# A ConvNeXt block and two Mamba layers on one core: a smaller first convolution group, ordered ahead of the weight preparation, and half of the first MLP moved into the stages

## The chip, the cores and the metric

The kernel runs on one core of one Trainium2 chip. A core has a matrix engine (TensorE, PE in the profile, with its weight loads as PEld), a vector engine (VectorE, DVE), a scalar engine (ScalarE, ACT) that evaluates functions such as exp or GELU from tables, a general engine (GpSimd, POOL) and a queue engine (SyncE, SP) that only issues DMA transfers. ACT and POOL can issue transfers too. Every engine takes its instructions in order and waits for the others through semaphores. The metric is the device time of one execution in microseconds; lower is better.

## What is computed

The input is `x` of 32 batches, 96 channels, 56 by 56 pixels, in fp32. Two layers follow each other.

```python
# layer 0, per batch
h = depthwise_conv7x7(x) + conv_b            # each channel with its own 7 x 7 filter
h = layernorm over the 96 channels
h = gelu(h @ w1 + b1) @ w2 + b2              # 96 -> 384 -> 96
x = x + layer_scale * h
# layer 1: two Mamba blocks over the 3136 pixels of a batch as a sequence
for i in range(2):
    xs, z = split(layernorm(seq) @ in_w[i])                  # 96 -> 2 x 192
    xc = silu(causal_conv4(xs))
    dt, Bm, Cm = split(xc @ xproj_w[i])                      # 6, 16, 16
    delta = softplus(dt @ dt_w[i] + dt_b[i])
    state = exp(delta * A) * state + delta * Bm * xc         # along the sequence, 192 x 16 states
    seq = seq + ((sum(state * Cm) + Dp * xc) * silu(z)) @ out_w[i]
# global branch, fusion, batch norm over all batches, and the residual
gp = relu(mean(x) @ gp_w.T + gp_b)
out = batchnorm(fus_w @ concat(seq, gp) + fus_b) + x
```

## The kernel before

**Front.** The depthwise convolution is done on PE. For a pair of channels, a banded matrix made of the filter (tile `band`, 112 rows by 7 times 128 columns) is multiplied with the padded image rows of the pair (`xpad`, 112 rows by batches by 62), in 7 matmuls, one per column shift, that add up in one PSUM bank. The bands are made by one trick: `line` (one row per channel, on DVE) is written 14 times over to `band_d` in DRAM (L137), and `load_band` (L154) reads it back with a row pitch one shorter than it was written. `conv_pair` issues the loads of `xpad` (L171) and `band`, the matmuls (L178), the evacuation to `ct` on ACT with the bias `cb` (L183) and the store to `conv_d` (L184). All these transfers are issued by SP. Three `band` and three `xpad` tiles rotate. The first group has 8 batches, so a matmul has 448 columns; its 48 pairs run in the front.

Between pair 2 and pair 3 stands, in the source, the preparation of the weights: small loads issued by POOL, products on DVE, three matmuls at L270 (`norm_weights`) and nine at L299 and L306, and two exponentials on ACT (`ar`, L327). The framework's scheduler orders the front itself, by its own estimates, so the order on an engine is not that of the source: on PE, L270, L299 and L306 stand ahead of the first conv pair. A transfer uses one of eight semaphores in turn (separately for POOL's and for those of SP and ACT), and waits until the transfer that had that semaphore before has landed.

Behind the conv comes the first MLP, for batch 0 alone: `block0(b, c, s)` is one half (392 pixels) of one chunk (784 pixels) of a batch, 8 halves a batch. In a half, the conv result `cv` is loaded (L417) and normalised (`center`, `square`, `mean`, `root`, `norm`: L379, L384, L389, L395/L396, L446), goes through both matrices with GELU between them (L451, L459, L467/L471), and the residual (L477) is stored to `x1_d` (L481). All eight halves of batch 0 run in the front from two pools of their own (`p0`, `pp0`), two halves at a time.

**Stages.** The rest is 256 stages, one for each layer, batch and chunk, in an order written out by hand (`manual_schedule`): layer 0 of a chunk, layer 0 of the next, layer 1 of the first, and so on. A stage has 24 steps; each step is an exponential on ACT (L918), a product with B (L900, DVE), a scan on DVE (L975), a product with C on POOL (L980), and matmuls that spread the input over the states (L947) and add the states up (L1021). Around the steps, pieces of other work are put by slot numbers, 24 slots a stage: `prep` of the next stage, `post` of the one before, one `block0` half of a later batch and one `conv` pair of a later group.

```python
        for m, S in enumerate(stages):
            ...
            if 2 <= m < len(halfs) + 2:
                put(m, block0(*halfs[m - 2]))
            if 2 <= m < len(convs) + 2:
                put(m, conv(*convs[m - 2]))
            if m + 1 < len(stages):
                put(m, prep(stages[m + 1]))
```

So conv pairs of the four later groups (6 batches each, 192 pairs) are in stages 2 to 193, and halves of batches 1 to 31 in stages 2 to 249. In a `conv` pair of a stage, loads are at slot -0.5, the taps (L565) at 5.4 to 10.2, the store at 11.8. A half loads `cv` at slot -6 and has its residual at 18.8. The matmuls of the first `prep` run ahead of the first step, and the first spread waits for the projection of the second stage's `prep` (L635), which stands in front of it on PE.

At the very end, statistics over all batches are reduced and the output is made from `o_d` and `x1_d` (the `fin` loop).

Of the kernel before, what the change touches and what calls it, by code (L numbers as in the profile page):

```python
# [34 lines left out]
F32 = mybir.dt.float32  # L35
# [7 lines left out]
H = W = 56  # L43
L = H * W
C = 96
# [6 lines left out]
NCH = 4  # L52
# [6 lines left out]
HP = 64  # L59
REP, PER = 14, 1024  # L60
# [3 lines left out]
def convnext_mamba_kernel(  # L64
# [31 lines left out]
    nc = tc.nc  # L96
    B = x.shape[0]

    dram = ctx.enter_context(tc.tile_pool(name="dram", bufs=1, space=DRAM))
    const = ctx.enter_context(tc.tile_pool(name="const", bufs=1))  # L100


    NB = 6
    b0 = B - 4 * NB if B > 4 * NB else B
    groups = [(0, b0)] + [(b, min(b + NB, B)) for b in range(b0, B, NB)]
    conv_d = [
        dram.tile([C * HP, (hi - lo) * W], F32, name=f"conv_d{lo}", tag=f"conv_d{lo}")
        for lo, hi in groups
    ]
    band_d = dram.tile([C, REP * PER], F32, name="band_d")  # L110
    stats_d = dram.tile([C, B * NCH, 4], F32, name="stats_d")
    x1_d = [dram.tile([C, L], F32, name=f"x1_d{b}", tag=f"x1_d{b}") for b in range(B)]
    o_d = [dram.tile([C, L], F32, name=f"o_d{b}", tag=f"o_d{b}") for b in range(B)]
# [3 lines left out]
    P2 = 2 * HP  # L117
    M2 = HP + H
    cb = const.tile([P2, C // 2], F32, name="cb")
    first_conv = ExitStack()  # L120
    cc = first_conv.enter_context(tc.tile_pool(name="cc", bufs=1))
    cx = first_conv.enter_context(tc.tile_pool(name="cx", bufs=3))
    cps = first_conv.enter_context(tc.tile_pool(name="cp", bufs=6, space=PSUM))
    cw = cc.tile([C, 49], F32, name="cw")
    nc.sync.dma_start(cw, conv_w)
    line = cc.tile([C, PER], F32, name="line")
    nc.vector.memset(line, 0.0)
    for dh in range(7):
# [3 lines left out]
            line.rearrange("p (k n) -> p k n", n=P2)[:, 0:7, HP + H + 2 - dh],  # L132
            cw[:, 7 * dh : 7 * dh + 7],
        )
    for lo in range(0, C, 24):
        r = slice(lo, lo + 24)
        nc.sync.dma_start(  # L137
            band_d[r].rearrange("c (r n) -> c r n", n=PER),
            line[r].unsqueeze(1).broadcast_to([24, REP, PER]),
        )  # L140
    nc.vector.memset(cb, 0.0)
    bv = conv_b.rearrange("(p two) k -> two p k", two=2)
    for j in range(2):
        nc.sync.dma_start(
            cb[j * HP : j * HP + H].unsqueeze(2), bv[j].partition_broadcast(H)
        )

    def load_band(T, p):

        for j in range(2):
            w = band_d[2 * p + j]
            nc.sync.dma_start(  # L154
                T[j * H : (j + 1) * H],
                bass.AP(
                    w.tensor, w.offset + HP + H - 1 - HP * j,
                    [[PER - 8, H // 8], [PER - 1, 8], [1, 7 * P2]],
                ),
            )  # L160

    bands, xpads = [], []
    for i in range(3):
        t = cc.tile([R2, 7 * P2], F32, name=f"band{i}", tag=f"band{i}")
        bands.append(t)
        t = cc.tile([R2, b0, W + 6], F32, name=f"xpad{i}", tag=f"xpad{i}")
        nc.gpsimd.memset(t, 0.0)
        xpads.append(t)
    def conv_pair(p):
        xp, T = xpads[p % 3], bands[p % 3]  # L170
        nc.sync.dma_start(  # L171
            xp[:, :, 3 : 3 + W],
            x[0:b0, 2 * p : 2 * p + 2, :].rearrange("b c (h w) -> (c h) b w", w=W),
        )
        load_band(T, p)
        ps = cps.tile([M2, b0 * W], F32, name="ps")
        for dw in range(7):
            nc.tensor.matmul(  # L178
                ps, T[:, dw * P2 : dw * P2 + M2], xp[:, :, dw : dw + W],
                start=(dw == 0), stop=(dw == 6),  # L180
            )
        ct = cx.tile([M2, b0 * W], F32, name="ct")
        nc.scalar.activation(ct, ps, AF.Identity, bias=cb[0:M2, p : p + 1])  # L183
        nc.sync.dma_start(conv_d[0][p * P2 : p * P2 + M2, :], ct)  # L184

    for p in range(3):
        conv_pair(p)


# [15 lines left out]
    for a in range(2):  # L205
        r = slice(64 * a, 64 * a + 64)
# [67 lines left out]
    for i in range(2):  # L274
# [12 lines left out]
        xp = blocks(xproj_w[i], f"xq{i}", su)  # L287
# [58 lines left out]
        nc.vector.memset(t[C : C + 1, :], 1.0)  # L346
        hn0s.append(t)

    for p in range(3, C // 2):
        conv_pair(p)  # L350
    first_conv.close()


    with ExitStack() as main:
        pre = []
# [49 lines left out]
        batch_sums = {}  # L405

        def block0(b, c, s):
            k = c * 2 + s
            v = {}

            def load():
                if k == 0:
                    batch_sums[b] = work([C, NCH * 2], "sums", 2)
                v["cv"] = work([C, ROWS, W], "cv", 1)
                g = 0 if b < b0 else 1 + (b - b0) // NB
# [97 lines left out]
        with tc.tile_pool(name="p0", bufs=1) as p0, tc.tile_pool(  # L513
            name="pp0", bufs=1, space=PSUM
        ) as pp0:
            pre += [p0, pp0]
            pieces = [
                (slot + 4 * c, piece)
                for c in range(NCH)
                for s in range(2)  # L520
                for slot, *_, piece in block0(0, c, s)
            ]
            for _, piece in sorted(pieces, key=lambda p: p[0]):
                piece()
            exp_ln_tables()
            pre.clear()
# [341 lines left out]
        stages = []  # L868
        for i, b, c in order:
            S = Stage()  # L870
            S.i, S.b, S.c, S.d, S.da, S.e, S.h, S.u4, S.pb = i, b, c, lay[i], {}, {}, {}, {}, {}
            stages.append(S)
        convs = [(g, p) for g in range(1, len(groups)) for p in range(C // 2)]
        halfs = [(b, c, s) for b in range(1, B) for c in range(NCH) for s in range(2)]

        def wide(k):

# [152 lines left out]
        def put(m, pieces):  # L1030
            for slot, *piece in pieces:
                where = slots if len(piece) == 1 else within
                where.setdefault(m * NSTEP + math.floor(slot), []).append((slot % 1, piece[-1]))
# [61 lines left out]
    with tc.tile_pool(name="sp", bufs=1) as sp:  # L1095
        n = B * NCH
# [21 lines left out]
    with tc.tile_pool(name="fin", bufs=4) as fin:  # L1118
        for b in range(B):
            for a in range(2):  # L1120
# [3 lines left out]
                r = fin.tile([C, 2 * CH], F32, name="fr")  # L1124
# [63 lines left out]
```

## Time and profile before

| | us |
|---|---|
| median of 3 executions | 15764.34 |
| lowest and highest | 15749.59, 15781.1 |
| the profiled execution | 15761.56 |
| its span in the profile | 15759.8 |

| engine | busy us | share |
|---|---|---|
| PE | 13461.7 | 85% |
| PEld | 5646.6 | 36% |
| DVE | 14771.9 | 94% |
| ACT | 11966.7 | 76% |
| POOL | 14367.3 | 91% |

The profile's page gives the busy time of each engine over the span, and rows of 40 equal slices (394 us each) in which a digit is the busy share in tenths. The timeline has one row per group of instructions: start in us, duration in us, engine, source line, operation, written tile, read tiles, shapes, count, and in brackets the idle time before it with what ended it. A row marked SPq is a transfer that SP's queue issued, and its duration is the time to issue it, with the time that the queue stood on it. A row of stretches gives the busy time of PE, PEld, DVE, ACT and POOL with the number of instructions, the granted TensorE clock (1.00 is full speed), the share of the 16 DMA engines' time, and GB/s.

### The profile page before, as it was taken

The numbers are of one execution on the slowest core, as the hardware profiler recorded it, in microseconds if no ns is written. First come the engines' busy times: TensorE is split into PE (matmuls) and PEld (weight loads), VectorE is DVE, ScalarE is ACT, GpSimd is POOL, SyncE is SP. The second block draws the span as 40 slices with busy tenths as digits, with TensorE's granted clock in tenths as the row PEclk, the third lists the DMA queues.
The fourth block names the chain that finished last, engine by engine and source line by source line (L and its number), as shares of the span: only waits on it lengthen the run. The fifth ranks groups of instructions, "written<-read, shape, count | busy, mean of one in ns | idle before, by whom it ended". The sixth has DMA issues, their size and how long they took to land. (4 is left out here: it accounts for less than half of the span.)

```text
span 15759.8 us, 207713 instructions
## 1 busy us (share of the span) xinstructions
PE 13461.7 (85%) x72120; PEld 5646.6 (36%) x72120; DVE 14771.9 (94%) x11457; ACT 11966.7 (76%) x23091; POOL 14367.3 (91%) x4746
## 2 busy tenths in 40 slices
PE   7798888888898898888898888998888888888870
PEld 3333333333333333333333333333333333333320
DVE  0799999999999999999999999999999999999993
ACT  1677778777878777787777787787777777777763
POOL 0799999999999999999999999999999999999990
PEclk9899999999999999999999999999999999999985
DMA  4454555555555545455554545545444444444438
GB/s 126 126 155 150 154 150 153 155 150 152 152 155 153 150 147 157 150 154 150 152 156 149 154 150 154 155 150 153 150 150 140 139 136 143 137 140 137 142 121 295
DMA packets 1304619, 2381.45 MB, mean 151 GB/s; under 512 B 490094, under 2 KB 699374, under 8 KB 1303564
## 3 DMA queue, kind: packets, MB, share of 16 engines
q1 hardware_dynamic: 1294108, 2327.73, 48.5%
q10 hardware_dynamic: 7168, 38.54, 0.6%
q8 instruction: 568, 9.31, 0.2%
q14 instruction: 487, 3.99, 0.1%
q0 software_dynamic: 2288, 1.88, 0.1%
HBM read 1973.83 MB, written 393.81 MB: 150 GB/s over the span
## 5 line engine op out<-in xcount | busy, mean ns | idle before, releaser
L980 POOL TENSOR_TENSOR h<-h,cp 128x1568 f32<-128x1568 f32 x3072 | 9939.7, 3251 | 547.1 <-DVE h L975 484.4
L975 DVE TENSOR_TENSOR_SCAN h<-da,w 128x785 f32<-128x785 f32 (+1 forms) x3072 | 5390.1, 1776 | 2.0 <-ACT da L918 2.0
L975 DVE TENSOR_TENSOR_SCAN h<-w,h 128x785 f32<-128x785 f32 (+1 forms) x3072 | 5287.1, 1769 | 73.0 <-ACT w L918 63.9
L957 POOL TENSOR_TENSOR h<-us,bp 128x1570 f32<-128x1570 f32 x1024 | 3323.7, 3246 | 73.3 <-PE y L1021 26.4
L918 ACT ACTIVATE w<-d,A 128x784 f32<-128x784 f32 x3072 | 2819.3, 918 | 576.9 <-DVE h L975 492.9
L900 DVE TENSOR_TENSOR w<-w,bp 128x786 f32<-128x786 f32 x3072 | 2916.4, 980 | 212.6 <-PE w L947 93.8
L918 ACT ACTIVATE da<-d,A 128x784 f32<-128x784 f32 x3072 | 2890.3, 947 | 12.4 <-DMA d<-dd 11.6
L1021 PE MATMUL y<-h,ssum 128*32 128x392 f32 x24576 | 2611.8, 516 | 39.7 <-POOL h L980 38.2
L635 PE MATMUL ps<-hn,wx 97*64 97x392 f32 x12288 | 2206.7, 501 | 22.0 <-POOL hn L626 22.0
L947 PE MATMUL w<-u,sel 64*128 64x393 f32 x4096 | 1002.0, 565 | 1173.9 <-DVE h L975 1160.1
L917 ACT COPY w<-st 128x1 f32<-128x1 f32 x2304 | 372.4, 162 | 1281.7 <-DVE h L975 1248.5
L565 PE MATMUL ps<-xpad,band 112*120 112x336 f32 x2688 | 1060.1, 512 | 331.4 <-ACT dl L708 331.4
L1021 PEld LDWEIGHTS y<-h,ssum 128*32 128x32 f32 x24576 | 698.6, 111 | 1724.1 <-issue 1488.3
L635 PEld LDWEIGHTS ps<-hn,wx 97*64 97x64 f32 x12288 | 813.8, 136 | 1348.5 <-issue 1291.5
L900 DVE TENSOR_TENSOR h<-w,bp 128x786 f32<-128x786 f32 x1024 | 990.5, 967 | 0.0
L375 ACT ACT_TABLE_LOAD x759 | 973.8, 1283 | 14.2 <-PEq L1175 0.7
L947 PEld LDWEIGHTS w<-u,sel 64*128 64x128 f32 x4096 | 327.2, 191 | 1565.8 <-DVE h L975 1140.8
L930 PEld LDWEIGHTS y<-sel 128*128 128x128 f32 x6144 | 747.1, 192 | 259.0 <-issue 97.0
L930 PE MATMUL y<-sel 128*128 128x120 f32 x6144 | 794.6, 279 | 21.1 <-DVE z L996 21.1
L384 ACT ACTIVATE sq<-ps 96x392 f32<-96x392 f32 x768 | 378.7, 493 | 557.6 <-PE ps L379 392.7
L565 PEld LDWEIGHTS ps<-xpad,band 112*120 112x120 f32 x2688 | 449.6, 191 | 935.2 <-ACT dl L708 446.5
L626 POOL TENSOR_TENSOR hn<-seq,hn 96x784 f32<-96x784 f32 x256 | 472.5, 1846 | 337.2 <-ACT hn L396 337.2
(158 smaller groups left out, 15975.4 us busy)
## 6 DMA issues: line engine op xcount, KB each, us to landing
d<-dd SPq DMA_DIRECT2D x1536, 392.0 KB
bp<-bd SPq DMA_DIRECT2D x1024, 392.0 KB
cp<-bd SPq DMA_DIRECT2D x1024, 392.0 KB
us<-uu SPq DMA_DIRECT2D x512, 392.0 KB
dd<-dl SPq DMA_DIRECT2D x512, 294.0 KB
band<-band_d SPq DMA_DIRECT2D x480, 196.0 KB
uu<-u SPq DMA_DIRECT2D x1024, 49.0 KB
cv<-conv_d SPq DMA_DIRECT2D x256, 147.0 KB
```

The costliest lines, as they stand in the source:

```text
L375: nc.scalar.preload_act_table_set("natural_log_exp_and_others")
L565: nc.tensor.matmul(v["ps"][0:M2, 0 : nb * W], band[:, dw * P2 : dw * P2 + M2], xpad[:, 0:nb, dw : dw + W], start=(dw == 0), stop=(dw == 6),)
L626: nc.gpsimd.tensor_tensor(hn, S.seq, hn, ALU.mult)
L635: nc.tensor.matmul(v["x", q][rows(a), 0:HC], weights[:, k, 64 * q : 64 * q + 64], v["hn"][:, o : o + HC], start=(k == 0), stop=(k == last),)
L900: nc.vector.tensor_tensor(halves(S.pb[j, g]), halves(S.u4[j])[:, :, 0 : HC + 1], halves(S.bc[0, g // 2][:, g % 2, :]), ALU.mult,)
L918: nc.scalar.activation(e[:, 1 : 1 + CH], S.d4[j], AF.Exp, scale=S.d["A"][:, j, g : g + 1])
L930: nc.tensor.matmul(spare, sel[:, 0, :], sel.rearrange("p a b -> p (a b)")[:, 0 : 512 - HC], start=True, stop=True,)
L947: nc.tensor.matmul(u4[:, 512 * a : 512 * a + HC + 1], sel[rows(a), j % 2, :], S.u[rows(a), j // 2, a : a + HC + 1], start=True, stop=True,)
L957: nc.gpsimd.tensor_tensor(states(S, j, h)[:, :, 0 : 1 + CH], S.us[j].unsqueeze(1).broadcast_to([128, 2, 1 + CH]), S.bc[0, h][:, :, 0 : 1 + ...
L975: nc.vector.tensor_tensor_scan(h[:, g % 2, at], S.e.pop((j, g))[:, at], S.pb.pop((j, g), h[:, g % 2, :])[:, at], 1.0 if c else 0.0, ALU.mu ...
L980: nc.gpsimd.tensor_tensor(h[:, :, 0:CH], h[:, :, 1 : 1 + CH], S.bc[1, g // 2], ALU.mult)
L1021: nc.tensor.matmul(S.y[r0 : r0 + 32, 0:HC], ssum, hs[k][:, g, tok(a)], start=False, stop=(half == 1 and g == 1),)
```

## The change

- The first group has 6 batches instead of 8; the later ones 6, 6, 7 and 7 instead of four of 6. A conv matmul of the front has 336 columns; one of the last two groups has 392.
- In the source, 24 conv pairs instead of 3 stand ahead of the weight preparation. After the other 24, the first five pairs of the second group run in the front too.
- `band` and `xpad` have six tiles each instead of three, `ct` six buffers instead of three.
- The bands are written in three parts: channels 0 to 7, 8 to 31 and 32 to 95, the last two when `conv_pair` comes to pairs 2 and 8.
- The bias `conv_b` is loaded as one row to all partitions (by ACT's queue) and sorted into `cb` by two DVE copies, instead of two loads of single elements by SP.
- The front's stores of `ct` are issued by ACT instead of SP.
- Of batch 0, four halves (chunks 0 and 1) of the MLP run in the front instead of eight. Half (0, 2, 0) is put into the `prep` of the first stage, halves (0, 2, 1) and (0, 3, 0) into stage 0, and (0, 3, 1) into stage 2. Each later half comes one stage later than before.
- The conv pairs of the stages start in stage 0 instead of stage 2: 187 pairs in stages 0 to 186.

```diff
-    NB = 6
-    b0 = B - 4 * NB if B > 4 * NB else B
-    groups = [(0, b0)] + [(b, min(b + NB, B)) for b in range(b0, B, NB)]
+    b0 = NB = min(6, B)
+    EARLY = 5
+    groups = [(0, b0)]
+    while groups[-1][1] < B:
+        lo = groups[-1][1]
+        groups.append((lo, min(lo + NB + (lo >= 3 * b0), B)))
+    NB = max(hi - lo for lo, hi in groups)
...
-    band_d = dram.tile([C, REP * PER], F32, name="band_d")
+    chunks = ((0, 8), (8, 32), (32, C))
+    band_d = [
+        dram.tile([hi - lo, REP * PER], F32, name=f"band_d{lo}", tag=f"band_d{lo}")
+        for lo, hi in chunks
+    ]
...
-    cx = first_conv.enter_context(tc.tile_pool(name="cx", bufs=3))
+    cx = first_conv.enter_context(tc.tile_pool(name="cx", bufs=6))
...
-    for lo in range(0, C, 24):
-        r = slice(lo, lo + 24)
+
+    def write_bands(k):
+        lo, hi = chunks[k]
         nc.sync.dma_start(
-            band_d[r].rearrange("c (r n) -> c r n", n=PER),
-            line[r].unsqueeze(1).broadcast_to([24, REP, PER]),
+            band_d[k].rearrange("c (r n) -> c r n", n=PER),
+            line[lo:hi].unsqueeze(1).broadcast_to([hi - lo, REP, PER]),
         )
+
+    write_bands(0)
+    brow = cc.tile([P2, C], F32, name="brow")
+    nc.scalar.dma_start(brow, conv_b.rearrange("c one -> one c").partition_broadcast(P2))
     nc.vector.memset(cb, 0.0)
-    bv = conv_b.rearrange("(p two) k -> two p k", two=2)
     for j in range(2):
-        nc.sync.dma_start(
-            cb[j * HP : j * HP + H].unsqueeze(2), bv[j].partition_broadcast(H)
+        nc.vector.tensor_copy(
+            cb[j * HP : j * HP + H],
+            brow[j * HP : j * HP + H].rearrange("q (p two) -> q p two", two=2)[:, :, j],
         )
...
-    for i in range(3):
+    NT = 6
+    for i in range(NT):
...
-    def conv_pair(p):
-        xp, T = xpads[p % 3], bands[p % 3]
+    def conv_pair(p, g=0):
+        lo, hi = groups[g]
+        i = (p + g * C // 2) % NT
+        xp, T = xpads[i], bands[i]
+        for k in range(1, len(chunks)):
+            if g == 0 and 4 * p == chunks[k][0]:
+                write_bands(k)
...
-        nc.sync.dma_start(conv_d[0][p * P2 : p * P2 + M2, :], ct)
-
-    for p in range(3):
+        nc.scalar.dma_start(conv_d[g][p * P2 : p * P2 + M2, :], ct)
+
+    for p in range(C // 4):
         conv_pair(p)
...
-    for p in range(3, C // 2):
+    for p in range(C // 4, C // 2):
         conv_pair(p)
+    for p in range(EARLY if len(groups) > 1 else 0):
+        conv_pair(p, 1)
     first_conv.close()
...
-                for c in range(NCH)
+                for c in range(2)
                 for s in range(2)
...
-        convs = [(g, p) for g in range(1, len(groups)) for p in range(C // 2)]
-        halfs = [(b, c, s) for b in range(1, B) for c in range(NCH) for s in range(2)]
+        convs = [(g, p) for g in range(1, len(groups)) for p in range(C // 2)][EARLY:]
+        halfs = [(b, c, s) for b in range(B) for c in range(NCH) for s in range(2)][7:]
...
-        for slot, *piece in sorted(prep(stages[0]), key=lambda p: p[0]):
+        for slot, *piece in sorted(
+            prep(stages[0])
+            + [(k - 6, *piece) for k, *piece in block0(0, 2, 0)],
+            key=lambda p: p[0],
+        ):
...
-            if 2 <= m < len(halfs) + 2:
+            if m == 0:
+                put(m, block0(0, 2, 1))
+                late = {-6: 15, 2: 19}
+                put(m, [(late.get(k, k + 8), *piece) for k, *piece in block0(0, 3, 0)])
+            elif 2 <= m < len(halfs) + 2:
                 put(m, block0(*halfs[m - 2]))
-            if 2 <= m < len(convs) + 2:
-                put(m, conv(*convs[m - 2]))
+            if m < len(convs):
+                put(m, conv(*convs[m]))
```

More of the change, by code (lines that the diff above doesn't have):

```diff
@@ L152, in load_band @@
         for j in range(2):
-            w = band_d[2 * p + j]
+            c = 2 * p + j
+            k = max(k for k in range(len(chunks)) if chunks[k][0] <= c)
+            w = band_d[k][c - chunks[k][0]]
             nc.sync.dma_start(
@@ L168, in convnext_mamba_kernel @@
         xpads.append(t)
-    def conv_pair(p):
-        xp, T = xpads[p % 3], bands[p % 3]
+    def conv_pair(p, g=0):
[5 more added lines that the diff above has]
+                write_bands(k)
         nc.sync.dma_start(
             xp[:, :, 3 : 3 + W],
-            x[0:b0, 2 * p : 2 * p + 2, :].rearrange("b c (h w) -> (c h) b w", w=W),
+            x[lo:hi, 2 * p : 2 * p + 2, :].rearrange("b c (h w) -> (c h) b w", w=W),
         )
@@ L412, in load @@
                 if k == 0:
-                    batch_sums[b] = work([C, NCH * 2], "sums", 2)
+                    batch_sums[b] = (
+                        const.tile([C, NCH * 2], F32, name="sums0")
+                        if pre
+                        else work([C, NCH * 2], "sums", 2)
+                    )
                 v["cv"] = work([C, ROWS, W], "cv", 1)
-                g = 0 if b < b0 else 1 + (b - b0) // NB
+                g = max(g for g in range(len(groups)) if groups[g][0] <= b)
                 at = (b - groups[g][0]) * W
```

## The prediction, made before the changed kernel was run

> **What bounds the kernel now.** I read the page's slices first. VectorE (DVE) and GpSimd (POOL) are at 9 tenths from the third slice on, and at 0 in the first. So there are two problems: a steady part with VectorE full, and a front in which it has nothing to do.
>
> ```profile
> DVE  0799999999999999999999999999999999999993
> POOL 0799999999999999999999999999999999999990
> ```
>
> The busy time by stretches (columns: PE, PEld, DVE, ACT, POOL, granted clock, DMA share, GB/s) gives the sizes. Up to 464.6 us VectorE works for 10 of the last 117 us; then come three stages of 56.7, 69.1 and 67.5 us; from the fourth on a stage is 57.7 us with 57.2 of VectorE. So the steady stage is VectorE's, and only the front and the first stages have time to give.
>
> ```profile
> 347.70:464.60 116.90, 89.65 (x306) 40.44 (x306) 9.91 (x16) 70.04 (x116) 9.58 (x4) 0.85 0.29 87
> 464.60:521.30 56.70, 28.75 (x145) 10.50 (x141) 56.18 (x43) 29.77 (x48) 46.96 (x15) 0.71 0.39 126
> 521.30:590.40 69.10, 50.77 (x258) 19.05 (x258) 57.19 (x44) 39.59 (x84) 55.32 (x20) 0.82 0.28 93
> 590.40:657.90 67.50, 59.90 (x328) 25.32 (x330) 57.17 (x45) 46.11 (x78) 57.04 (x20) 0.92 0.48 145
> 657.90:715.60 57.70, 51.47 (x286) 21.82 (x282) 57.16 (x45) 47.98 (x104) 56.02 (x19) 0.97 0.53 159
> ```
>
> The timeline of the front, engine by engine, says what each piece waits for.
>
> ```profile
> 2.02 14.58 SPq L144 DMA_DIRECT2D cb<-in_conv_b  x2
> 16.65 19.36 SPq L171 DMA_DIRECT2D xpad<-in_x  x1
> 36.06 8.77 SPq L137 DMA_DIRECT2D band_d<-line  x4
> ...
> 40.72 0.51 POOL L225 DMA_DIRECT2D bng<-in_bn_g  x1 [11.53 <-DMA w_sb<-in_w]
> ...
> 81.78 1.57 PE L270 MATMUL ps<-raw,m 96*97 96x384 f32 x2 [25.11 <-DMA raw<-in_in_w]
> 85.86 0.55 PE L299 MATMUL ps<-ident,ow 64*96 64x64 f32 x2 [2.52 <-DMA ow<-in_out_w]
> ...
> 327.08 0.64 ACT L183 ACTIVATE ct<-ps,cb 120x448 f32<-120x448 f32 x1 [4.68 <-PE ps L178]
> 332.39 0.63 ACT L183 ACTIVATE ct<-ps,cb 120x448 f32<-120x448 f32 x1 [4.68 <-PE ps L178]
> ...
> 354.03 2.90 PE L379 MATMUL ps<-cv,center_m 96*96 96x392 f32 x4 [5.78 <-DMA cv<-conv_d]
> ```
>
> TensorE (PE) does the weight preparation first, waits for weights that POOL's queue loads (until 85.9), and begins the convolution at 90.06. That then runs without a gap, a pair of channels each 5.31 us (332.39 - 327.08), to 347.7. The first MLP (L379 on) starts 6.3 us later, behind the store and reload of the result. In front of all, SP's queue stood behind the two loads of `cb` until 36 us, and POOL's weight loads stood too.
>
> **The change, part by part.** The built order of instructions settles one thing: on PE the three L270 matmuls and the L299/L306 ones still stand ahead of the first conv pair, and on ScalarE (ACT) the two exponentials of `ar` do. So the conv does not overtake the weights on PE; it starts when they are done, only sooner.
>
> *Start of the conv.* The elementwise `cb` loads leave SP (a row load on ACT's queue and two VectorE copies instead, off the path), and only 32 of 96 rows of bands are written at once. POOL issues 52 loads up to the last `ow`. From 53.5 to 81.3 it issued 24 in 27.9 us, 1.16 each, beside the band write; free of waits one takes about 0.6 (0.51 to 0.71 in the rows). The early bands, six pairs of loads and SP's waits for earlier landings should keep the queues busy to some 33 us: from 4.5 us, 25 loads at 1.16 and 27 at 0.6 end at 50, and landing and the PE/VectorE chain (81.33 to 90.06 before: about 8) end at 57 or 58. I take 57: -33. Bounds: all at 0.6 gives 44 (-46); all at 1.16 gives 73 (-17).
>
> *The conv.* 48 pairs of 448 columns become 53 of 336. In a steady stage four 336-column matmuls last 1.40 us and two 0.82, so 0.29 each, 14 per pair: 4.06; 5.31 x 336/448 gives 3.98. I take 4.0: 53 x 4.0 = 212, plus 2.7 for the cold start that it has now (257.6 - 48 x 5.31), plus a stall. The stall: the last 64 rows of bands (3.67 MB) are written from SP after pair 7's loads; at the rate of the write before (5.5 MB from 39 to 77 us in the packets) that is 25 us, and pair 9's band load waits for an earlier DMA's landing in that order, about 41 us after the conv's start where PE wants it at 36: 5 us (0 to 15). 219.7 against 257.6: -38. The DMA share of 0.55 over 5.31 is 2.9 us of all engines per pair, less with 6 batches, so under 4.0. The store goes to ACT's queue: ACT waited 4.68 of each 5.31, so its issue is covered.
>
> *From conv to MLP.* `cv` of batch 0 needs the first 48 pairs, and five more follow, 20 us: its store and load are covered. The gap of 6.3 becomes 0.5: -5.8 (0 if a buffer holds it).
>
> *Two of four chunks of the first MLP leave.* Last results of chunk 3 came at 406.5; those of chunk 1 come 4.7 us behind its last GELU at 377.3, as chunk 3's did (401.8 to 406.5): 382.0. -24.5.
>
> *One half (0,2,0) goes into the first stage's preparation*, on ACT between Softplus and the next norm, which L635 and through it the first spread and scan wait for.
>
> ```profile
> 439.03 1.54 ACT L708 ACTIVATE dl<-ps,dtb 128x392 f32<-128x392 f32 x3
> 441.40 0.49 ACT L384 ACTIVATE sq<-ps 96x392 f32<-96x392 f32 x1 [0.82 <-PE ps L379]
> ...
> 443.22 1.28 ACT L395 ACT_TABLE_LOAD   x1
> 444.51 0.55 ACT L395 ACTIVATE ps<-ps,eps_c 96x392 f32<-96x392 f32 x1
> ```
>
> Its square, root, GELU, residual and 3 table loads are 0.5 + 1.05 + 1.5 + 0.8 + 3 x 1.28 = 7.7 us of ACT; the PE steps between them, at the cold clock here, about 4: +11.6. Here a rule speaks against the change: the Trainium skill ("ScalarE: Activation LUTs", What ACT_TABLE_LOAD costs) prices a switch at about 2.66 us, 1.28 load and 1.38 drain. The rows show the next activation 0.01 us behind the load's end (443.22 + 1.28 = 444.50), and no drain. By the row 3 loads are 3.8 us, by the rule 8.0, and the part +15.8. I take the row.
>
> *First stages.* Stage 0 gains two halves and a conv pair: about 15 us of ACT and 16 of PE against 29.8 and 28.8 busy of 56.7. It fits, but at a clock of 0.71 and in in-order queues; stages 1 and 2, which have 21 us of waits between them, get conv pieces in front of the post-projection that stage 2 hangs on. +8 (0 to 25).
>
> *Steady part.* Counting the gates by L996 (565 in 10932 us, 182 in 3558, three a stage): 58.05 us a stage with conv, 58.65 toward the end, where there is none. Conv ends 7 stages earlier: +3. The last two groups have 7 batches, 14 matmuls of 0.33 for 0.28, 0.66 us of PE in each of 96 stages; PE is busy 51.5 of 57.7 and VectorE sets the stage: 0. At three group borders the reload of `cv` stands 6 slots of 2.4 us, 15 us, behind the last store: 0 (up to 5 each).
>
> Sum: -33 - 38 - 5.8 - 24.5 + 11.6 + 8 + 3 = -78.7 against the span of 15759.8. What lies outside the span (1.8 us) stays. The profiled execution was 15761.6, 2.8 under the median, so against the median 15764.3 I get 15685.
>
> **Rivals.** *The front is held by DMA.* For: the weights and the early bands share 16 engines, and 8 outstanding loads wait for one another. Weights end at 73 (-17), a conv pair takes 4.6 (-11 with the stall), the gap stays, table switches cost the rule's price, stages lose 15: -17 - 11 - 24.5 + 15.8 + 15 + 3 = -19, 15745. Against: conv ran gapless at a DMA share of 0.55. Chance 0.14, half of it under 31 us of gain.
>
> *All cover holds.* Weights issue-bound (-46), no stall (-43), no loss in the stages: -46 - 43 - 5.8 - 24.5 + 11.6 + 3 = -105, 15659. Chance 0.12.
>
> *Slower.* PE's queue in stages 91 to 186: the wider conv taps stand ahead of the spread L947, which VectorE's L900 waits for. At half clock the 0.66 us are 1.3; fully exposed, 96 x 1.3 = +126, and -79 + 126 = +47: 15811. It decides from 79 / 96 = 0.82 us a stage. Against: in the stage of 57.7 us VectorE idles half a us, and stages with conv are no slower than those without. Chance 0.06.
>
> **How the numbers follow.** The likeliest case has 0.68: 15685, its own range 15652 to 15718 from the ends of the start, the stall and the stages, not all at once. The range 15640 to 15740 adds most of the better case and the better half of the DMA case, and leaves out the slower one. A measurement of this kernel tells some 0.2% (32 us) from no change. Faster: 0.68 + 0.12 + 0.07 = 0.87; within: 0.07; slower: 0.06.
>
> **What would show it.** PE's first conv matmul near 57 us; evacuations of `ct` 4.0 us apart, with one gap near pair 9; the last near 276; the first L379 within 1 us of it; VectorE's first L900-type multiply near 375 for 464.6; the stages after the fourth at 57.7 to 58.2, with seven-batch ones alike. Wrong it goes if `ct` comes at 4.5 us or more, if the weights end after 75, or if the stage's length moves by 0.3 us.

## The result, and the profile after

| | before | after |
|---|---|---|
| median of 13 executions, us | 15764.34 | 15728.87 |
| lowest and highest | 15742.7, 15781.1 | 15707.89, 15739.37 |
| profiled execution, its span | 15761.56, 15759.8 | 15707.89, 15706.1 |

The changed kernel takes 0.9977 of the time before, with a 95% interval of 0.9969 to 0.9986: 35 us less, where 79 were forecast. The profiled execution is the fastest of its 13, so its span shows 53.7 us of gain. A second profile of the same kernel (`e3_again` below, span 15726.3, near the median) shows 33.5. Both are used here.

In the slices of the page the front shrinks: the second slice, at 7 tenths before, is full, and the first has some work.

```profile
DVE  1999999999999999999999999999999999999993
POOL 1899999999999999999999999999999999999990
```

The timeline of the changed kernel answers the rows of the front (start, duration, engine, line, operation, count, and the idle time before it with its releaser):

```profile
49.17 1.59 PE L291 MATMUL ps<-raw,m 96*97 96x384 f32 x2 [11.93 <-DVE m L289]
52.27 0.55 PE L320 MATMUL ps<-ident,ow 64*96 64x64 f32 x2 [1.50 <-DMA ow<-in_out_w]
...
56.78 41.77 PE L199 MATMUL ps<-xpad,band 112*120 112x336 f32 x140
100.58 173.59 PE L199 MATMUL ps<-xpad,band 112*120 112x336 f32 x602 [2.02 <-DMA band<-band_d]
...
266.22 0.54 ACT L204 ACTIVATE ct<-ps,cb 120x336 f32<-120x336 f32 x1 [3.45 <-PE ps L199]
270.22 0.54 ACT L204 ACTIVATE ct<-ps,cb 120x336 f32<-120x336 f32 x1 [3.45 <-PE ps L199]
...
274.20 1.45 SPq L444 DMA_DIRECT2D cv<-conv_d  x3
276.74 1.87 PE L402 MATMUL ps<-cv,center_m 96*96 96x392 f32 x4 [2.57 <-DMA cv<-conv_d]
...
340.30 1.28 ACT L418 ACT_TABLE_LOAD   x1
...
342.00 0.56 ACT L418 ACTIVATE ps<-ps,eps_c 96x392 f32<-96x392 f32 x1 [0.41 <-PE ps L412]
342.57 1.28 ACT L419 ACT_TABLE_LOAD   x1
343.86 0.47 ACT L419 ACTIVATE ps<-ps 96x392 f32<-96x392 f32 x1
...
376.65 0.98 DVE L927 TENSOR_TENSOR w<-w,bp 128x786 f32<-128x786 f32 x1 [31.72 <-PE w L974]
```

The conv starts at 56.78, has one stall of 2.02 us behind its tenth pair (140 matmuls), evacuates a pair each 4.00 us and ends at 274.2. The first MLP begins 2.6 us later, and VectorE's first multiply is at 376.65 instead of 464.57: 87.9 us sooner. All of the front's forecast is there. Where the rest went, the busy time by stretches says. I cut at the gates on VectorE (L996 before, L1023 after): up to the first of stage 3, and from the first of stage 4 to the first of stage 250. The columns are the stretch, its length, then busy time of PE, PEld, DVE, ACT and POOL, granted clock, DMA share, GB/s. Before:

```profile
0.00:689.85 689.85, 522.95 (x1879) 232.82 (x1880) 230.26 (x246) 243.55 (x429) 238.56 (x141) 0.92 0.43 122
747.54:15058.66 14311.12, 12647.88 (x68701) 5301.60 (x68699) 14056.92 (x10856) 11366.31 (x22075) 13769.10 (x4490) 0.94 0.49 149
```

After:

```profile
0.00:609.93 609.93, 489.79 (x1956) 251.56 (x1957) 230.05 (x246) 241.37 (x428) 239.45 (x144) 0.90 0.48 138
667.63:15008.00 14340.37, 12705.09 (x68595) 5286.93 (x68594) 14057.34 (x10855) 11366.69 (x22065) 13771.89 (x4491) 0.94 0.49 149
```

| us | before | after | after, second profile |
|---|---|---|---|
| start to stage 3 | 689.85 | 609.93 (-79.9) | 616.40 (-73.5) |
| stages 4 to 249 | 14311.1 | 14340.4 (+29.3) | 14350.6 (+39.5) |
| stage 3, stages 250 to the end | 758.8 | 755.8 (-3.0) | 759.3 (+0.5) |
| span | 15759.8 | 15706.1 (-53.7) | 15726.3 (-33.5) |

VectorE, GpSimd and ScalarE are busy as long as before in the stages (14057 us of VectorE in both), so the 29 to 39 us are waits of an engine that is nearly full. Most of them sit in one place. The length of a stage by its number m modulo 8 (from the gates, mean over stages 4 to 186; eight stages are one batch). The first gate of a stage is at its slot 13, so a length counted between gates runs from slot 13 of a stage to slot 13 of the next:

| m mod 8 | 0 | 1 | 2 | 3 | 4 | 5 | 6 | 7 |
|---|---|---|---|---|---|---|---|---|
| before | 57.98 | **59.02** | 57.68 | 57.95 | 57.90 | 57.92 | 57.89 | 58.32 |
| after | 57.96 | 57.69 | **60.41** | 57.99 | 58.18 | 57.93 | 57.84 | 58.06 |

One stage in eight was long before, by 1.1 us. Now it is the next one, and it is long by 2.5. The two columns give -1.33 + 2.73 = +1.40 per eight stages, which over 246 stages would be +43; added up directly over stages 4 to 249 they give +36 (+40 in the second profile). The stages with m = 4 add 6 (12), and those with m = 7 give back 17 (19), most of it behind stage 186, where no conv is left.

What is in that stage is the last half of a batch. It carries, beside its MLP, the pooled branch: `total` (a sum on DVE), `pool` and `fuse` (each two one-column matmuls on PE and a small activation on ACT), at slots 21.5, 29.4 and 30.4 counted from the half's own stage, so the two of PE and ACT fall at slots 5.4 and 6.4 of the stage behind it, which is still in front of that stage's first gate and so counts to the half's own stage in the table. The change puts every half one stage later, and the pooled branch with it: from stages 9, 17, ... to stages 10, 18, .... The timeline of the changed kernel there, in stage 42 (61.26 us long), all engines in order of time:

```profile
2927.36 0.48 PE L517 MATMUL ps<-mean,gpw_sb 96*96 96x1 f32 x2 [2.38 <-ACT dl L735]
2929.41 0.48 PE L523 MATMUL ps<-gp,fw 96*96 96x1 f32 x2 [0.26 <-ACT gp L519]
...
2931.00 3.05 PE L826 MATMUL ps<-seq,fw 96*96 96x392 f32 x4
...
2932.12 0.25 ACT L529 ACTIVATE fb<-ps,fusb 96x1 f32<-96x1 f32 x1
2932.43 0.40 PEld L826 LDWEIGHTS ps<-seq,fw 96*96 96x96 f32 x2 [1.14 <-ACT fb L529]
...
2933.98 3.94 PE L832 MATMUL ps<-z,ow 64*96 64x392 f32 x12
2937.95 0.58 ACT L846 ACTIVATE seq<-ps,fb 96x392 f32<-96x392 f32 x1 [2.37 <-PE ps L832]
2938.72 0.92 ACT L945 ACTIVATE w<-d,A 128x784 f32<-128x784 f32 x1
2939.67 3.48 DVE L1002 TENSOR_TENSOR_SCAN h<-w,h 128x785 f32<-128x785 f32 x2 [1.98 <-ACT w L945]
```

PE stands 2.38 us for ACT's softplus (`dl`) in front of the first small product, and 0.26 for ACT's `gp` in front of the second. Behind them comes the projection of the stage before (L826, L832). `fuse` and the projection use the same PSUM tile (`ps1`, one buffer), so the projection's third and fourth matmul wait until ACT has read it for `fb` (1.14 us on the weight load). The projection ends at 2937.92; ACT has an activation for its result (L846) ahead of the next exponential and stands 2.37 us; VectorE's scan stands 1.98 us for that exponential. The same place of the kernel before, one stage sooner in the order (stage 41, 58.94 us long):

```profile
2936.53 0.48 PE L496 MATMUL ps<-gp,fw 96*96 96x1 f32 x2 [1.05 <-ACT gp L492]
...
2938.12 2.82 PE L799 MATMUL ps<-seq,eye 96*96 96x392 f32 x4
2938.99 0.25 ACT L502 ACTIVATE fb<-ps,fusb 96x1 f32<-96x1 f32 x1
2940.87 3.05 PE L805 MATMUL ps<-z,ow 64*96 64x392 f32 x12
2943.95 0.49 ACT L813 ACTIVATE seq<-ps 96x392 f32<-96x392 f32 x1 [1.51 <-PE ps L805]
2944.34 0.91 ACT L918 ACTIVATE w<-d,A 128x784 f32<-128x784 f32 x1
```

There the projection that follows is layer 0's. It has the same four first matmuls (L799) and stands behind `fb` too, but ACT waits only 1.51 for its result. Two differences show in the rows. From the start of ACT's activation to the next exponential are 0.39 us there, and 0.77 in the changed kernel: layer 1's result takes an accumulator read besides, and the stage then running carries a state over, so that a copy stands before each exponential. And the twelve matmuls of the projection take 3.05 us there and 3.94 here. The granted clock over them was 0.72 before; in the changed kernel it was 0.56 in stage 42, and 0.82 in stage 50, which is 59.02 us long (these rows count the twelve matmuls alone: length, PE, PEld, granted clock, DMA share, GB/s):

```profile
2940.87:2943.92 3.05, 3.04 (x12) 1.30 (x12) 0.72 0.85 282
2933.98:2937.92 3.94, 3.94 (x12) 1.54 (x12) 0.56 0.91 291
3400.72:3403.40 2.68, 2.68 (x12) 1.16 (x12) 0.82 0.95 301
```

So the mean of 60.41 hides two kinds of stage. The trace records the granted clock as stretches at full and at half speed. Every one of these stages has one half-speed stretch over the small products and the projection, of either 6.8 or 10.2 us. In stages 9 to 185, number of stages and their mean length:

| | 6.8 us at half clock | 10.2 us at half clock |
|---|---|---|
| before, m = 1 | 21, 58.82 | 2, 61.12 |
| after, m = 2 | 11, 59.65 | 11, 61.20 |
| after, second profile | 9, 59.70 | 13, 61.17 |

With the longer stretch the twelve matmuls take 4.2 us in the mean, with the shorter one 2.8 to 2.9. Some 0.8 us of the +1.40 are there at the same 6.8 us of half clock; the rest goes with the longer stretch, which has become common. What lengthens it, and which comes first, the wait or the clock, no run separates.

The waits of VectorE between 2000 and 11000 us (what it waited for: total us, times, longest) say the same: before

```profile
DVE h L975 <- ACT w L918: 20.2, 33, 2.5
DVE w L900 <- PE w L947: 18.4, 21, 1.2
```

and after

```profile
DVE h L1002 <- ACT w L945: 41.0, 34, 2.6
DVE w L927 <- PE w L974: 32.9, 57, 0.9
```

The scan's wait for ACT is doubled, in hardly more places. So the theory to be tested (A in the expectations) is: the shift of the halves by one stage moves the pooled branch to a stage in which it costs more, and that eats a third to a half of the front's gain. Of its rivals there, B and D put the loss in other work that the change moves (the wider conv groups, the halves themselves), and C in the scatter between executions.

### The profile page after: what moved, and what is told of

Read it like the earlier page. It is cut to its first block, busy times and chain, and to the rows that moved or that the text cites. A ratio compares the mean times of both kernels' runs of the same rounds, so it can differ in the third digit from the quotient of the medians.

```text
span 15706.1 us, 207665 instructions
## 1 busy us (share of the span) xinstructions
PE 13487.0 (86%) x72120; PEld 5655.2 (36%) x72120; DVE 14772.8 (94%) x11459; ACT 11973.0 (76%) x23094; POOL 14371.2 (92%) x4749
## 3 DMA queue, kind: packets, MB, share of 16 engines
q14 instruction: 487, 3.99, 0.1%
## 5 line engine op out<-in xcount | busy, mean ns | idle before, releaser
L592 PE MATMUL ps<-xpad,band 112*120 112x336 f32 (+1 forms) x2618 | 1122.9, 547 | 318.2 <-ACT dl L735 318.2
L832 PE MATMUL ps<-z,ow 64*96 64x392 f32 x3072 | 763.9, 643 | 0.0
```

Source lines behind the costliest of these rows:

```text
L592: nc.tensor.matmul(v["ps"][0:M2, 0 : nb * W], band[:, dw * P2 : dw * P2 + M2], xpad[:, 0:nb, dw : dw + W], start=(dw == 0), stop=(dw == 6),)
L832: nc.tensor.matmul(v["ps"][a][0:C, 0:HC], S.d["ow"][rows(a), q, :], S.z[rows(a), q, :], start=False, stop=(q == NQ - 1),)
```

## The experiments

Each was timed beside the kernel before, on the same chip in the same minutes. The chip is one for `e1` to `e4`, another for `e6` to `e9`, a third for `e10` and `e11`; between these groups the ratios are compared, not the medians.

**The halves back in their old stages (`e1_align`).** One more conv pair runs in the front, and half (0, 3, 1) goes into stage 1, so that from stage 2 on every half stands where it stood before.

```diff
-    EARLY = 5
+    EARLY = 6
...
-        halfs = [(b, c, s) for b in range(B) for c in range(NCH) for s in range(2)][7:]
+        halfs = [(b, c, s) for b in range(B) for c in range(NCH) for s in range(2)][8:]
...
+            elif m == 1:
+                late = {-6: -1, 2: 4}
+                put(m, [(late.get(k, k), *piece) for k, *piece in block0(0, 3, 1)])
-            elif 2 <= m < len(halfs) + 2:
+            elif m < len(halfs) + 2:
```

> The changed kernel with half (0,3,1) of the first MLP in stage 1, so that every later half stands in the stage that it had before the change (six early conv pairs instead of five, +4 us in the front, so that the second group is ready a stage sooner). Theory A, the shift by one stage: the two one-column matmuls of the pooled branch, once a batch, now stand in front of the post-projection of a stage with more ACT work; the trace of the changed kernel shows 60.4 us for that stage against 59.0 before, 1.4 x 31 = 43 us. Then this run takes 4 - 43 = 39 us off the changed kernel: about 15690, and the stages of 61 us are gone. Theory B, the seven-batch conv groups make the stages longer: nothing changes but +4, about 15733. Theory C, the medians differ by run-to-run scatter alone: 15733 too.

Measured: 15710.78 us (15695.58 to 15714.91), 0.9962 of before (0.9949 to 0.9974). Stages 4 to 249, by stretch:

```profile
690.90:14998.90 14308.00, 12660.22 (x68590) 5279.98 (x68588) 14056.34 (x10856) 11367.23 (x22068) 13775.54 (x4491) 0.94 0.49 149
```

14308.0 is what the kernel before takes (14311.1), 32 to 43 less than after; stages with m = 1 mod 8 are at 59.13 again (mean over stages 4 to 186), and all others between 57.7 and 58.2. This is A's number for the stages. The total is 20 above A's all the same, because the edit costs elsewhere: the half in stage 1 makes the first stages longer. VectorE's rows there:

```profile
489.07 0.56 DVE L473 TENSOR_TENSOR hz<-cv,ps 96x392 f32<-96x392 f32 x1 [8.09 <-ACT ps L419]
498.77 0.98 DVE L927 TENSOR_TENSOR w<-w,bp 128x786 f32<-128x786 f32 x1 [5.76 <-PE w L974]
511.27 1.79 DVE L1002 TENSOR_TENSOR_SCAN h<-da,w 128x785 f32<-128x785 f32 x1 [5.35 <-ACT da L945]
```

The gate of stage 3 comes at 633.5, 17 to 24 later than after. The last six stages and the final pass over the output are 12 to 16 longer too; of that 7 to 10 lie in the final pass, which the edit doesn't touch, and no cause was found.

**The shift alone, in the kernel before (`e2_shift`).**

```diff
-            if 2 <= m < len(halfs) + 2:
-                put(m, block0(*halfs[m - 2]))
+            if 3 <= m < len(halfs) + 3:
+                put(m, block0(*halfs[m - 3]))
```

> The kernel before with nothing changed but the halves of batches 1 to 31, which come one stage later (stages 3 to 250), as in the changed kernel. Theory A: +1.4 us in one stage of eight, +43 us in all: about 15807. Theories B and C: 15764, no difference.

Measured: 15837.18 us (15830.03 to 15838.63), 1.0043 of before (1.0029 to 1.0056): slower by 70, more than A said. The sign and the place are A's: stages with m = 2 mod 8 take 60.57 (mean over stages 4 to 186). But 14377.0 us in the stages are 66 above before, and A's step explains 1.4 x 31 = 43. The rest is in stages with m = 4 mod 8, at 59.00 where before has 57.90. VectorE's scans wait 75.9 us for ACT between 2000 and 11000 us, after 20.2 in the kernel before:

```profile
DVE h L975 <- ACT w L918: 75.9, 61, 2.6
```

**The changed kernel again (`e3_again`).** No edit; a second profile.

> The changed kernel once more, for a second profile. Its first profile is the fastest of 13 executions (15708 against a median of 15729). If the scatter sits in the stages, this profile has the same front (first scan multiply at 376.5 us, 88 us before that of the kernel before) and stages that are some 20 us longer in sum; if it sits in the front, the stages agree and the front differs. Median about 15729.

Measured: 15729.91 us (15713.89 to 15742.23), 0.9977 (0.9968 to 0.9986).

```profile
0.00:616.40 616.40, 494.25 (x1956) 252.11 (x1957) 230.05 (x246) 241.33 (x428) 239.30 (x144) 0.90 0.48 136
674.10:15024.70 14350.60, 12718.76 (x68595) 5287.24 (x68594) 14058.42 (x10855) 11366.00 (x22065) 13772.17 (x4490) 0.94 0.49 149
```

The front is 6.5 us longer in this execution and the stages 10. Part of the 10 is again in stages with m = 4 mod 8: the six between stages 43 and 91 take 59.10 in the mean, where the first profile has 57.68. One by one they take 57.7, 59.0 to 59.2, or 62.0 us; the stage of 62.0 has 17.1 us at half clock, those of 57.7 have 3.4. So one program falls in one or the other pattern from execution to execution; what decides it stays open. It does not lie wholly beside the step between old and new place: over stages 4 to 249 the stages with m = 4 take 58.15 to 58.74 in the five profiles with the pooled branch one stage later (both of after, e2, e6, e8) and 57.94 to 58.07 in the four with it in its old place (before, e1, e9, e10). The sums of stages 4 to 249 keep the two sets apart all the same: 14340 to 14377 us in the five, 14297 to 14318 in the four.

**The pooled branch out of the kernel (`e7_nopool`).** In the changed kernel the fused bias becomes the constant one and the three pieces go; the output then lacks the pooled term.

```diff
-            last = [(21.5, total), (29.4, pool), (30.4, fuse)] if k == 2 * NCH - 1 else []
+            batch_bias[b] = fusb
+            last = []
```

> The changed kernel without the pooled branch: no sum over a batch, no two one-column matmuls with their activations; the bias of the fusion alone is added (so the output lacks the pooled term). Theory A: the longest stage of eight, 60.4 us, falls to the 58.0 of the others, 2.4 x 31 = 75 us: 15654. Rival D, that stage is longer for where the halves of the first MLP stand and not for the pooled branch: it stays at 60.4, and the median at 15729.

Measured: 15661.16 us (15650.79 to 15683.73), 0.9944 (0.9932 to 0.9957): 68 under the changed kernel's median, 52 by the two ratios ((0.9977 - 0.9944) x 15764), near A's number and far from D's.

```profile
669.10:14950.70 14281.60, 12672.71 (x68488) 5275.64 (x68485) 14050.94 (x10824) 11358.52 (x22008) 13770.72 (x4490) 0.94 0.50 150
```

14281.6 us, 59 to 69 under after, with the gate of stage 3 where it was (610.4), and no stage in eight stands out (means over stages 4 to 186 between 57.7 and 58.4; m = 2 has 58.16). Without the branch the projection's twelve matmuls start 1.9 to 3.6 us behind the softplus there (m = 2, stages 10 to 178), with it some 6.1. So this branch, 0.96 us of PE a batch, costs (14311 - 14282) / 31 = 0.9 us a batch in its old place and, 30 times in these stages, 2.0 to 2.3 in its new one.

**The branch one stage later, the halves not (`e8_tail24`).** As e1, and:

```diff
-            last = [(21.5, total), (29.4, pool), (30.4, fuse)] if k == 2 * NCH - 1 else []
+            last = [(21.5, total), (53.4, pool), (54.4, fuse)] if k == 2 * NCH - 1 else []
```

> The run with the halves in their old stages (15711 us), with only the pooled branch's two matmuls and activations 24 slots, one whole stage, later: they stand in the stage in which the changed kernel has them, and all else where the kernel before had it. Theory A (the pooled branch in the wrong stage is the loss): its stages become as long as the changed kernel's, +30 to +40: 15741 to 15751. Rival D (the shift of the halves is the loss): 15711.

Measured: 15746.62 us (15738.59 to 15755.51), 0.9993 (0.9985 to 1.0001), inside A's bracket.

```profile
684.10:15033.60 14349.50, 12727.14 (x68585) 5293.44 (x68583) 14056.97 (x10856) 11367.41 (x22066) 13770.43 (x4491) 0.94 0.49 149
```

e1 and e8 differ in two slot numbers: 14308.0 and 14349.5 us, and the latter is what the changed kernel has (14340.4 and 14350.6). By the ratios e8 is (0.9993 - 0.9962) x 15764 = 49 us slower, clear of both intervals. The long stage is m = 2 mod 8 again, at 60.73 (stages 4 to 186; 15 of its 22 up to stage 178 have the 10.2 us at half clock). This run decides where the loss of the stages comes from: the place of the pooled branch alone, not that of the halves, their loads or their conv results, and not the wider groups. Why that place is dearer is read from the rows above, not tested apart.

**The branch half a stage later (`e4_tail`).** As e1, with `pool` at 38.5 and `fuse` at 40.5.

> The first of these runs, with the two one-column matmuls of the pooled branch moved from slots 29.4 and 30.4 to 38.5 and 40.5, behind the post-projection of the next stage instead of in front of it. Theory A: the stage with the pooled branch loses its excess over the others too, 1.1 us x 31 = 34 us less than the first run: about 15656. If the pooled branch is not the cause of that excess, the same as the first run, about 15690.

Measured: 15763.14 us (15748.38 to 15784.69), 0.9998 (0.999 to 1.0006): a miss by both theories, 52 above e1. Its stages take 14364.2 us, and two in eight are long (m = 2 and 3 mod 8, 60.28 and 59.87 over stages 4 to 186). From stage 187 on, where there is no conv, the two are at 58.9 and 57.8. The projection is no longer late here (ACT waits 0.0 and 0.3 us for it in the mean of these stages), so this loss does not come the way that the changed kernel's does. These slots lie on both sides of the next half's `up` and `gelu` (15 and 15.2), behind the conv taps; that they meet in a PSUM tile was argued and not tested. The clock goes with the length again: stages with m = 3 take 57.7 us with 3.4 at half clock, 59.0 to 59.3 with some 6.2, and 62.2 to 62.9 with 17.1.

**The front in the order of the source (`e6_order`).** PE and ACT follow the source from the first conv pair to the last one of the front, so the conv really stands ahead of the weight preparation.

```diff
+    in_order = ExitStack()
+    in_order.enter_context(tc.manual_schedule(engines={mybir.EngineType.PE, mybir.EngineType.Activation}))
     for p in range(C // 4):
         conv_pair(p)
...
         conv_pair(p, 1)
+    in_order.close()
     first_conv.close()
```

> The changed kernel with PE and ACT held to the order of the source in the front, so that 24 conv pairs really stand ahead of the weight preparation on both. Theory: the conv of the changed kernel starts at 56.8 us because PE waits there for the last weights; its own first loads are issued by 25.6 us, so it starts near 26 and, with some 5 us more of waits for the band writes, ends 25 us sooner: median 15729 - 25 = 15704. Rival: the front is held by the transfers of bands and images (5.5 MB of bands and 0.7 MB a pair); then the first pair starts early but the last evacuation stays near 274 us, and the median at 15729.

Measured: 15705.88 us (15696.69 to 15724.98), 0.9971 (0.996 to 0.9982): 23 under the changed kernel's median, but only 0.0006 or some 10 us by the ratios, whose intervals overlap. PE's rows:

```profile
29.53 34.33 PE L199 MATMUL ps<-xpad,band 112*120 112x336 f32 x112 [29.53 <-DMA band<-band_d]
72.35 67.04 PE L199 MATMUL ps<-xpad,band 112*120 112x336 f32 x224 [8.49 <-DMA band<-band_d]
...
146.11 1.57 PE L293 MATMUL ps<-raw,m 96*97 96x384 f32 x2 [5.43 <-DMA raw<-in_in_w]
...
151.97 118.41 PE L199 MATMUL ps<-xpad,band 112*120 112x336 f32 x406
```

The conv starts 27 us sooner and ends at 270.4, 4 us sooner: 8.5 us go to a wait for bands, and the weights, now in the middle of it, still make PE wait 5.4. So the profile speaks for the rival and the median for the theory. The profiled execution was the slowest of the seven (15724.98). What the order alone is worth stays unclear.

**Six halves in the front, none in the first preparation (`e9_six`).** Halves (0, 2, 0) and (0, 2, 1) go back to the front, the two of chunk 3 into stage 0, a sixth conv pair into the front, and from stage 2 on all stands as before.

```diff
-    EARLY = 5
+    EARLY = 6
...
-                for c in range(2)
+                for c in range(3)
...
-            + [(k - 6, *piece) for k, *piece in block0(0, 2, 0)],
...
-                put(m, block0(0, 2, 1))
-                late = {-6: 15, 2: 19}
-                put(m, [(late.get(k, k + 8), *piece) for k, *piece in block0(0, 3, 0)])
+                put(m, block0(0, 3, 0))
+                late = {-6: 15, 2: 19, 29.4: 53.4, 30.4: 54.4}
+                put(m, [(late.get(k, k + 8), *piece) for k, *piece in block0(0, 3, 1)])
```

(and `[8:]` in `halfs`).

> Six halves of batch 0 in the front (three chunks), none in the first stage's preparation, halves (0,3,0) and (0,3,1) in stage 0, so that every later half stands in its old stage, and six early conv pairs. Against the changed kernel: one chunk more in the front +12.1, no half in the preparation -12.9, one more early pair +4, the stages -35 as in the run with the old stages: 15729 - 32 = 15697.

Measured: 15682.57 us (15676.57 to 15690.8), 0.9956 (0.9943 to 0.997).

```profile
671.70:14968.90 14297.20, 12706.22 (x68589) 5285.15 (x68587) 14056.32 (x10856) 11358.48 (x22068) 13771.03 (x4491) 0.94 0.49 149
```

By the ratios that is 33 us under the changed kernel, where 32 were expected. The stages keep the aligned length (14297.2) and the gate of stage 3 is at 614, between the two profiles of after. So the halves that moved into the first preparation and stage 0 gave little: two of them back in the front cost no more there than they saved here.

**e9 with e6's order (`e10_both`).**

> Six halves of batch 0 in the front with every later half in its old stage (15683 us), and PE and ACT in the source's order in the front. The profile of the run with that order alone shows its conv only 4 us sooner at the end, its median 23 us lower. If the profile is right: 15679; if the median is: 15660.

Measured: 15675.72 us (15672.48 to 15694.48), 0.995 (0.9938 to 0.9963). By the ratios some 9 us under e9, within what the intervals leave open, so the order of the front is worth little beside it.

**e10 with the branch 3.8 slots later (`e11_tail9`).**

```diff
-            last = [(21.5, total), (29.4, pool), (30.4, fuse)] if k == 2 * NCH - 1 else []
+            last = [(21.5, total), (33.2, pool), (34.3, fuse)] if k == 2 * NCH - 1 else []
```

(and batch 0's branch by as much).

> The last one with the pooled branch's two matmuls at slots 33.2 and 34.3, just behind the post-projection's two moves, instead of 29.4 and 30.4 in front of it. If standing in front of the post-projection is what costs, the stage with the pooled branch loses its excess of some 1.1 us, 31 times: 34 us less than the run beside it. If any place between the conv's taps costs the same, no difference; at slots 38.5 and 40.5 it cost 50 us more.

Measured: 15660.9 us (15651.99 to 15681.04), 0.9939 (0.9925 to 0.9952).

```profile
667.60:14956.30 14288.70, 12654.80 (x68585) 5276.64 (x68583) 14054.43 (x10856) 11366.79 (x22066) 13773.14 (x4491) 0.95 0.50 149
```

Stages with m = 1 mod 8 fall from 59.37 (e10) to 58.34 (means over stages 4 to 186), and ACT no longer stands for the projection there (1.67 us a stage in e10, none here). The stages together fall from 14317.9 to 14288.7, 7 us above those without the branch at all. The medians differ by 15 us only, their intervals overlap, and e10's profiled execution was the slowest of its five: 34 were expected, and how much of it this place brings stays open. This kernel computes all of the output. It is 98 us under the kernel before in the same comparison (15759.31), and by the ratios 60 under the changed one.

## Why the prediction was wrong

| step, us | predicted | measured |
|---|---|---|
| start of the conv | -33 (at 57) | -33.3 (at 56.78) |
| the conv, with its stall | -38 | -40.2 |
| from conv to MLP | -5.8 | -3.8 |
| two of four chunks leave | -24.5 | -23.7 |
| one half in the first preparation | +11.6 | +12.9 |
| first stages | +8 | +8.0 |
| steady part | +3 | +29.3, and +39.5 |
| the end | 0 | -3.0, and +0.5 |

The rows of the front are those of the first profile; between the second and third of them lies 0.2 us more of unchanged preparation, so they sum to -79.9. The second profile's front gives -73.5, 3.8 of the difference in the conv.

- *Start of the conv: right.* The weights still stand ahead of it on PE (L291, L320), as the built order said.
- *The conv: right.* A pair takes 3.99 to 4.00; the stall is at the tenth pair and 2.0 (2.7 in the second profile) instead of 5.
- *From conv to MLP: right in direction, short by 2.* The cover was there for the store, but SP issued the `cv` loads only when the conv ended (274.20), and PE waited 2.57 for them.
- *The half in the first preparation: right.* Softplus to first multiply is 38.43 us for 25.54. The table switch cost what the row of before had said: the activation before ends at 342.56, the load is at 342.57 and 1.28 long, and the next activation starts at 343.86. The Trainium skill's 2.66 ("ScalarE: Activation LUTs", What ACT_TABLE_LOAD costs) would have asked for 1.36 more than the 1.30 between the two activations.
- *First stages: right.*
- *Steady part: this is the step that failed.* It read "Conv ends 7 stages earlier: +3", and priced the wide conv taps and the reload at the borders at 0. The +3 should have been 7 x (58.65 - 58.05) = 4.2 by its own figures, and did not come: stages 187 to 193 take 405.4 us without conv, for 407.0 with it. Both zeros held: from stage 91 to 186, where groups have 7 batches, an eight-stage mean of after is 58.2 with its long stage, and 58.3 before stage 91, with 6; and the stages at the borders (42, 90 and 138: 61.0 to 61.6) are like others of their place. What it left out is a line of the change's own list: each later half comes one stage later. The prediction has no term for it, so it stood at nothing without a reason. But a half's last pieces meet whatever stands in the stage they fall in, and a chain of PE, ACT, PE, ACT with one column at a time went from 0.9 to 2.0 or 2.3 us a batch. In place of +3 the stages took 29.3 and 39.5 us more. Of the step in that stage's mean (+1.40), some 0.6 go with the longer half-speed stretches of the clock. e8 shows that those slots alone do it, e2 that the shift does it without the rest of the change, e7 that without the branch nothing is lost.
- *Range and rivals.* The measured 15729 is in the range, but only because that reaches towards the DMA rival (15745), and not by its mechanism: weights, pair and stall all came in at or under their terms. The slower rival named the right kind of place, an in-order queue of PE in the steady stages, and the wrong resident: the conv taps cost nothing.
- *What would have shown it.* The trace of before has a long stage in eight (59.02), which a mean of 58.05 a stage hides. Cut by eight, the gates would have pointed at the stage of the last half, and its rows at `pool` and `fuse`.

## What to carry to other kernels

When work that repeats is shifted by one slot in an order written by hand, cost its smallest pieces too: read the stage lengths by their place in the period, find the long one, and ask what its odd pieces will stand beside after the shift. What a product of one column costs is set by what stands behind it in the in-order queues: 0.96 us of matmul a batch cost from next to nothing to 2.8 us here, by slot. Look at the single stages too, with the granted clock beside them: a mean can be a mixture of two lengths. And when a front gets shorter, check that the loop behind it keeps its phase.

## What the runs showed of the hardware that was not expected

- Two pairs of one-column products at three places in schedules that are otherwise e1's made stages 4 to 249 take 14308.0 (slots 29.4 and 30.4), 14349.5 (53.4 and 54.4) and 14364.2 us (38.5 and 40.5); without them the changed kernel takes 14281.6. That is up to 2.8 us a batch. At 33.2 and 34.3, with six halves in the front, it was 14288.7; that is 7 us above the kernel without them, and two profiles of one kernel differ by 10. VectorE's busy time does not show it (14056 to 14057 us in the first two and in after).
- The granted TensorE clock stood at half speed for stretches of 3.4, 6.8 or 10.2 us in the stages (two of 13.7), and the length of a stage goes with them: one and the same place of the period took 59.0 to 60.0 us with 6.8 and 60.8 to 61.4 with 10.2 (after, m = 2), or 57.7 with 3.4 and 62.0 with 17.1 in two stretches (m = 4). Which one a stage gets changes from one execution to another; what selects it is open.
- The final pass over the output, the same code in all kernels, took 361 to 374 us from the last gate to the end, with no order that follows the edits.
